# Halved query scaling, held token scaling and an earlier channel mix in a four-layer network

## The chip, the cores and the metric

The kernel runs on one core of one Trainium2 chip. The metric is the device time of one execution in microseconds (us); before the change the median of three runs is 1311.0.

## The reference

`x` is 8 batches of 256 tokens of 256 features, the context 8 batches of 256 tokens of 192 features. All is fp32.

```python
x = x + xattn0(layernorm(x), ctx, mask)     # 16 heads of 16
x = x + soft_moe(layernorm(x))              # 8 experts of 128 slots, hidden 1024, gelu
# second attention, 16 heads of 64:
h = layernorm(x)
q, k, v = h @ w_q, ctx @ w_k, ctx @ w_v     # 256 -> 1024, 192 -> 1024
x = x + softmax(q k^T / 8) v @ w_out + b_out
# channel mix:
h = layernorm(x)
prev = h shifted by one token (zero first)
xr = mu_r * h + (1 - mu_r) * prev
xk = mu_k * h + (1 - mu_k) * prev
x = x + sigmoid(xr @ W_r^T) * (relu(xk @ W_k^T) ** 2 @ W_v^T)
```

## The kernel before

Tokens lie on the 128 partitions: batch b is token tiles 2b and 2b+1 of the resident buffer `x_sb`. The stages follow one another: the first attention, the soft mixture of experts (until 866 us), the second attention (866 to about 1231 us) and the channel mix (to the end), with the later stages' first steps drawn into the earlier ones.

The first stages are left alone by the diff. The experts' matmuls `ph` (L1237) and `pe` (L1253) take turns, ACT reads `ph` (L1245), and the last matmuls `pc` (L1279) are added to `x_sb` by DVE (L1287). Then SP issues the loads of the weights of the last two layers (L1344 to L1359), at the very end the two small loads of `mu`, from which DVE makes `omu` = 1 - mu (L1361).

The second attention is a pipeline by steps. A step is one pair of heads of one batch, 64 steps in all; two steps make a group, and 36 rounds n = 0 to 35 run the 32 groups: `stage(k, g)` issues part k of group g. Part 0 is the scores and DVE's row maximum `nm` and ACT's exponentials `ex`; part 1 the reciprocal `rz` on DVE and the multiplication of `ex` on POOL (L1512); part 2 the transposes `pe` and their copies `et` (L1529, alternately by DVE and ACT); part 3 the products with V; part 4, after a batch's last step, the projection `po`. In a round, parts 3, 2 and 1 of earlier groups are issued in that order around two lists of extra pieces, `between[n]` and `ahead[n]`, written out by hand: for batch b, `normed_of(b)` scales the tokens with their mean and root (`xh_l`, two DVE operations of L106), `turned_of(b)` transposes them (`pt_x`, copied to `xT`) and adds the output bias to `x_sb` on POOL (L1411), `queries_of(b, t2)` makes the queries of four heads, `keys_of` and `values_of` the keys and values.

A query piece, `q_piece`, is four matmuls into one PSUM tile `pq` of 128x512 (one of three buffers of that size that all such tiles share): two for heads t = 2 t2 and two for t = 2 t2 + 1, each with 256 columns. Each fp32 matmul shows as two passes in the profile. Then one DVE operation (L1429) scales all 512 columns into `QT`. There are 32 such pieces.

Order within an engine: all matmuls and transposes are kept in program order. On DVE, ACT and POOL a scheduler may move an operation ahead of others if it is not marked. `Ordered` is a wrapper of DVE and POOL, used by `normed` and by the iterated roots: what is issued through it while `Ordered.held` is true keeps its place in program order. In before this was so for the tokens of channel mix batches 0 and 1 and the iterated roots, not for `xh_l`.

The channel mix of batch b has five pieces, `mixes[b][0]` to `[4]`: [4] scales the tokens (`xh_ffn`), [0] transposes them (`pt_xf`) and blends them with their shifted copy by `mu` on ACT (L1636) and `omu` on DVE (L1639), [1] makes the keys (`pk`), [2] the gates (`pr`, sigmoid on ACT), [3] the values (`pv`), the product, the addition of `x_sb` and the store. Roots of the variances: batches 0 to 3 by a Newton iteration (`first_roots`), batches 4 to 6 by ACT's square root and a DVE reciprocal (`mix_roots`, L1750), batch 7 by iteration (`last_roots`).

Of the kernel before, what the change touches and what calls it, by code (L numbers as in the profile page):

```python
# [15 lines left out]
P = 128  # L16
# [50 lines left out]
def kernel(ctx: ExitStack, tc: tile.TileContext, a: dict, out: bass.AP):  # L67
# [1266 lines left out]
    with ExitStack() as l1:  # L1334
# [61 lines left out]
        def proj1(b):  # L1396

            to = {}  # L1400

            def normed_piece():
                mv, rstd = xat_stats[b // 2]
                to["xh"] = normed(b, mv, rstd, "l1", of=4)

            def xt_piece():
                pt = transposed(to["xh"], f"x1_{b}", transpose)
                to["xT"] = p1.tile([P, 2, S], F32, tag="xT", bufs=1, name=f"xT1_{b}")
                nc.vector.tensor_copy(to["xT"], pt)
                for t in range(2):  # L1410
                    nc.gpsimd.tensor_tensor(  # L1411
                        x_sb[:, 2 * b + t, :], x_sb[:, 2 * b + t, :], bo, ALU.add
                    )

            def q_piece(t2):
                if t2 == 0:
                    to["QT"] = p1.tile([P, 8, S], F32, tag="QT", bufs=2, name=f"QT1_{b}")
                pq = ps_mm(f"q1_{b}_{t2}").rearrange("p (t n) -> p t n", t=2)
                for i in range(2):
                    t = 2 * t2 + i  # L1420
                    for c in range(2):
                        matmul(
                            pq[:, i, :],
                            lhsT=wq[:, c, t * P : (t + 1) * P],
                            rhs=to["xT"][:, c, :],
                            start=(c == 0),
                            stop=(c == 1),
                        )
                nc.vector.tensor_scalar(  # L1429
                    to["QT"][:, 2 * t2 : 2 * t2 + 2, :], pq, HD1**-0.5, None, ALU.mult  # L1430
                )

            def values_of(u):

                if u == 0:
                    to["V"] = p1.tile([P, 2, DA], F32, tag="V", bufs=2, name=f"V1_{b}")
                pv = [ps_mm(f"v1_{b}_{u}_{h}") for h in range(2)]
                t0 = S * b + u * P
                cols = [slice(h * 512, (h + 1) * 512) for h in range(2)]
                for h in range(2):  # L1440
                    matmul(
                        pv[h],
                        lhsT=ctx0T[:, t0 : t0 + P],
                        rhs=wv[:, 0, cols[h]],
                        start=True,
                        stop=False,
                    )

                def halves():
                    for h in range(2):  # L1450
                        r = slice(64 * h, 64 * h + 64)
                        matmul(
                            pv[h],
                            lhsT=ctx1T[r, t0 : t0 + P],
                            rhs=wv[r, 1, cols[h]],
                            start=False,
                            stop=True,
                        )
                    nc.scalar.copy(to["V"][:, u, cols[0]], pv[0])
                    nc.vector.tensor_copy(to["V"][:, u, cols[1]], pv[1])  # L1460

                return halves

            return (
                to,
                [lambda t=t: q_piece(t) for t in range(4)],
                [lambda u=u: values_of(u) for u in range(2)],
                normed_piece,
                xt_piece,
            )  # L1470
# [122 lines left out]

        normed_of(0)()
        turned_of(0)()
        normed_of(1)()
        keys_of(0, 0)()
        queries_of(0, 0)()
        xat_stats[3] = ln_pair(3, "xat_3")
        keys_of(0, 1)()  # L1600
        queries_of(0, 1)()
# [14 lines left out]
        def channel_mix(b):  # L1616
            xh = []

            def mix_normed():
                mv, rstd, of = ffn_stats[b]  # L1620
                Ordered.held = b < 2
                xh.append(normed(b, mv, rstd, "ffn", of=of))
                Ordered.held = False

            def mix():
                if b >= 2:
                    mix_normed()
                st = homes[b % 2]
                yT = yTs[b % 2]
                pt = transposed(xh[0], f"xf_{b}", transpose)  # L1630
                nc.vector.tensor_copy(yT[:, :, 1 : S + 1], pt)
                for k, n in enumerate(("r", "k")):
                    m = st[n].rearrange("p (c n) -> p c n", c=2)
                    for c in range(2):
                        i = 2 * k + c
                        nc.scalar.activation(  # L1636
                            m[:, c, :], yT[:, c, 1 : S + 1], AF.Copy, scale=mu[:, i : i + 1]
                        )
                        nc.vector.scalar_tensor_tensor(  # L1639
                            m[:, c, :],  # L1640
                            yT[:, c, 0:S],
                            omu[:, i : i + 1],
                            m[:, c, :],
                            ALU.mult,
                            ALU.add,
                        )
# [95 lines left out]
            root_step(rstd, v, t)  # L1742
            Ordered.held = False

        def mix_roots(b, of):

            mv, rstd = halves[b // 4]
            part = slice(2 * b % 8, 2 * b % 8 + 2 * of)
            tc.keep_in_program_order(
                nc.scalar.activation(rstd[:, part], mv[:, part, 1], AF.Sqrt, bias=epsb)  # L1750
            )
            nc.vector.reciprocal(rstd[:, part], rstd[:, part])

        def last_roots(b):

            mv, rstd = halves[b // 4]
            part = slice(2 * b % 8, 2 * b % 8 + 2)
            v = stat.tile([P, 8], F32, tag="nv", bufs=1, name=f"nv_ffn_{b}")[:, :2]
            Ordered.held = True
            vec.tensor_scalar(v, mv[:, part, 1], EPS, None, ALU.add)  # L1760
            inverse_root(rstd[:, part], v, f"ffn_{b}")
            Ordered.held = False
# [1 line left out]
        mixes = [channel_mix(b) for b in range(B)]  # L1764
        between = {n: [] for n in range(len(groups) + 4)}
        ahead = {n: [] for n in range(len(groups) + 4)}
        between[1] += [keys_of(0, 2), queries_of(0, 2), queries_of(0, 3), turned_of(1)]
        between[2] += [queries_of(1, 0)]
        ahead[2] += [keys_of(0, 3), values_of(0, 0), values_of(0, 1)]
        between[3] += [queries_of(1, 1)]  # L1770
        ahead[3] += [keys_of(1, 0)]
        between[4] += [queries_of(1, 2), queries_of(1, 3), normed_of(2), turned_of(2)]
        ahead[4] += [keys_of(1, 1), values_of(1, 0)]
        between[5] += [queries_of(2, 0), queries_of(2, 1)]
        ahead[5] += [keys_of(1, 2), values_of(1, 1)]
        between[6] += [queries_of(2, 2)]
        ahead[6] += [normed_of(3), keys_of(1, 3), values_of(2, 0)]
        between[7] += [queries_of(2, 3), turned_of(3)]
        ahead[7] += [values_of(2, 1)]
        for n in range(8, len(groups)):  # L1780
            b, i = n // 4 + 1, n % 4
            if b < B:
                between[n].append(queries_of(b, i))
            if i == 3 and b + 1 < B:
                between[n].append(turned_of(b + 1))
            if i == 2 and b + 1 < B:
                ahead[n].append(normed_of(b + 1))
            if i < 2 and n // 8 < B // 2 - 1:
                ahead[n].append(keys_of(n // 8 + 1, n % 8 // 4 * 2 + i))
            elif i >= 2 and b < B:  # L1790
                ahead[n].append(values_of(b, i - 2))
        for n in range(len(groups) + 4):
# [3 lines left out]
            for piece in between[n]:  # L1796
                piece()
            for k in (1, 2) if n < 28 else (2, 1):
                stage(k, n - k, slice(1, 2))
            if n - 4 != 27:  # L1800
                stage(4, n - 4)
            for piece in ahead[n]:
# [3 lines left out]
                mix_stats(n // 4 - 2, n % 4)  # L1806
            if 22 <= n < 25:
                first_roots(n - 22)
            if n in (30, 31):
                mixes[n - 30][4]()  # L1810
            if n == 32:
                homes_of_mix()
                mixes[0][0]()
                stage(4, 27)
                mixes[1][0]()
                for t in range(2):
                    mix_stats(6, t)
                mix_roots(4, 3)
            if n == 33:
                mixes[0][1]()  # L1820
                mixes[0][2]()
            if n == 34:
                mixes[1][1]()
        for t in range(2):
            mix_stats(7, t)
        last_roots(7)
        mixes[1][2]()
        for b in range(2, B + 2):
            if b < B:
                mixes[b][0]()  # L1830
            if 3 <= b <= B:
                mixes[b - 1][1]()
                mixes[b - 1][2]()
            mixes[b - 2][3]()
# [62 lines left out]
```

## Time and profile before

| | us |
|---|---|
| median of 3 runs | 1311.0 (1310.98 to 1312.02) |
| profiled execution | 1311.15 |
| its span | 1309.0 |
| busy PE | 1288.0, 98% of the span |
| busy ACT, DVE | 583.8 and 568.7 |
| busy POOL | 264.6 |
| granted PE clock, mean | 0.999 |

The span is the profiled part of the execution; 2.15 us lie around it. PE is the tensor engine's matmuls, PEld its weight loads, DVE the vector engine, ACT the scalar engine, POOL the general engine, SP the engine that issues the loads and stores. A row of the timeline gives the start, the duration, the engine, the line of the kernel, the operation, output and inputs, partitions by elements, how often it follows on itself, and in brackets the idle time of the engine ahead of it with what ended it. A row of groups gives busy time and mean ns of one, then idle time ahead and its main cause.

### The profile page before, as it was taken

What the parts mean: (1) busy time and instruction counts of PE and PEld (TensorE: products, weight loads), DVE (VectorE), ACT (ScalarE), POOL (GpSimd) and SP (SyncE); (2) the same over time, 40 slices, a digit from 0 to 9 for tenths busy, and PEclk for the clock granted to TensorE, in tenths of its full rate; (3) what the DMA queues carried; (4) which work ended last, traced back from release to release, by engine and by line L of the source; (5) the groups of instructions that cost most, each with busy time, mean ns of one, the idle gap of its engine ahead of it and who ended that gap; (6) DMA issues with size and microseconds to landing.
All of it is one profiled execution on the core that took longest, in us unless ns stands there. A gap on an engine that the chain in (4) does not pass through costs nothing.

```text
span 1309.0 us, 19001 instructions
## 1 busy us (share of the span) xinstructions
PE 1288.0 (98%) x7459; PEld 943.0 (72%) x7459; DVE 568.7 (43%) x1121; ACT 583.8 (45%) x1425; POOL 264.6 (20%) x322
## 2 busy tenths in 40 slices
PE   9999999999999999999999999999999999999998
PEld 6656555676778787787877888875666677677777
DVE  6778767243310333303333010035545535544855
ACT  4755556363521445414443232224445445544843
POOL 4563112110100010000101000023334233233523
PEclk9999999999999999999999999999999999999999
DMA  7001000242442332334322344250000000000001
GB/s 217 7 1 34 33 1 2 101 137 69 137 136 72 135 137 69 105 101 137 111 95 71 135 137 139 102 157 1 1 1 1 1 1 1 1 1 1 2 9 57
DMA packets 59144, 86.84 MB, mean 66 GB/s; under 512 B 3248, under 2 KB 49200, under 8 KB 59056
## 3 DMA queue, kind: packets, MB, share of 16 engines
q1 hardware_dynamic: 58560, 85.18, 19.8%
q8 instruction: 59, 0.97, 0.3%
q10 hardware_dynamic: 496, 0.46, 0.1%
q14 instruction: 29, 0.24, 0.1%
HBM read 83.53 MB, written 2.10 MB: 65 GB/s over the span
## 4 chain that ended last, share of the span: by engine, by line
PE 91%; ACT 4%; DVE 3%; POOL 1%; DMA 1%; issue 1%; SPq 0%; ACTq 0%; DVEq 0%; POOLq 0%
PE ph L1237 17%; PE pe L1253 16%; PE sc L77 9%; PE o L77 6%; PE po L77 6%; PE q L77 5%; PE v L77 5%; PE pe L80 4%; PE pc L1279 4%; PE k L77 4%; PE ln L1101 3%; PE pf L1183 3%; PE ln L77 1%; PE pk L77 1%; ACT ex L652 1%; PE pf L77 1%
## 5 line engine op out<-in xcount | busy, mean ns | idle before, releaser
L1245 ACT ACTIVATE ht<-ph,b 128x256 f32<-128x256 f32 x256 | 119.3, 474 | 377.1 <-PE ph L1237 371.7
L1237 PE MATMUL ph<-slots,w 128*128 128x256 f32 x1024 | 266.6, 384 | 1.2 <-ACT ht L1245 0.6
L1253 PE MATMUL pe<-w,ht 128*128 128x256 f32 x1024 | 263.2, 381 | 0.0
L1237 PEld LDWEIGHTS ph<-slots,w 128*128 128x128 f32 x1024 | 182.4, 189 | 53.8 <-ACT ht L1245 21.5
L1253 PEld LDWEIGHTS pe<-w,ht 128*128 128x128 f32 x1024 | 192.1, 190 | 29.9 <-DVE slots L1262 4.2
L1512 POOL TENSOR_TENSOR ex<-ex,rz 128x1024 f32<-128x1024 f32 x64 | 120.4, 1897 | 233.4 <-DVE rz L1510 200.4
L1499 ACT ACTIVATE ex<-sc,nm 128x256 f32<-128x256 f32 x256 | 117.4, 484 | 52.1 <-DVE nm L1494 50.4
L1161 POOL TENSOR_TENSOR es<-es,zs 128x1024 f32<-128x1024 f32 x12 | 22.7, 1895 | 429.6 <-DVE zs L1160 429.6
L652 ACT ACTIVATE ex<-sc 128x512 f32<-128x512 f32 x128 | 75.3, 598 | 65.2 <-PE sc L77 57.6
L1262 DVE TENSOR_TENSOR slots<-pe,b 128x512 f32<-128x512 f32 x32 | 22.1, 692 | 185.1 <-PE pe L1253 185.1
L106 DVE TENSOR_REDUCE NM<-sc 128x2 f32<-128x512 f32 x128 | 86.7, 688 | 23.0 <-PE sc L77 19.3
L77 PE MATMUL sc<-KT,QT 64*128 64x256 f32 (+2 forms) x896 | 93.7, 380 | 0.7 <-DVE NM L106 0.5
L77 PEld LDWEIGHTS sc<-KT,QT 64*128 64x128 f32 (+2 forms) x896 | 69.5, 186 | 20.6 <-issue 13.2
L1494 DVE TENSOR_REDUCE nm<-sc 128x4 f32<-128x1024 f32 x64 | 75.4, 1220 | 7.8 <-PE sc L77 4.2
L77 PE MATMUL po<-wo,ot 128*128 128x256 f32 x320 | 73.5, 384 | 0.3 <-ACT et L1529 0.3
L80 PE MATMUL pe<-ident,ex 128*128 128x128 f32 x512 | 69.0, 278 | 1.9 <-DVE et L1529 1.9
L80 PEld LDWEIGHTS pe<-ident,ex 128*128 128x128 f32 x512 | 56.6, 141 | 18.5 <-issue 13.7
L77 PEld LDWEIGHTS po<-wo,ot 128*128 128x128 f32 x320 | 59.5, 190 | 12.1 <-issue 2.7
L77 PE MATMUL o<-et,V 128*64 128x256 f32 x512 | 62.3, 385 | 0.0
L77 PE MATMUL q<-xT,wq 128*128 128x256 f32 x256 | 60.4, 381 | 0.0
L1279 PE MATMUL pc<-slots,CT 128*128 128x256 f32 x256 | 57.5, 379 | 0.0
L1499 ACT ACTIVATION_READ_ACCUMULATOR ex<-sc,nm 128x1 f32 x256 | 55.2, 216 | 0.0
(259 smaller groups left out, 1708.0 us busy)
## 6 DMA issues: line engine op xcount, KB each, us to landing
w<-in_w_dram SPq DMA_DIRECT2D x64, 1024.0 KB, 6.3
b<-in_b_dram SPq DMA_DIRECT2D x32, 128.0 KB, 6.7
x_sb<-in_x_dram SPq DMA_DIRECT2D x3, 512.0 KB, 7.8
se<-in_slots_dram SPq DMA_DIRECT2D x1, 1024.0 KB, 11.8
wq<-in_wq_dram SPq DMA_DIRECT2D x1, 1024.0 KB, 4.7
wo<-in_wo_dram SPq DMA_DIRECT2D x1, 1024.0 KB, 11.3
ctx1T<-in_ctxT_dram SPq DMA_DIRECT2D x7, 128.0 KB, 7.0
ctx0T<-in_ctxT_dram SPq DMA_DIRECT2D x3, 256.0 KB, 7.3
```

Source lines behind the costliest of these rows:

```text
L77: tc.keep_in_program_order(nc.tensor.matmul(out, lhsT=lhsT, rhs=rhs, start=start, stop=stop))
L80: tc.keep_in_program_order(nc.tensor.transpose(out, in_, ident))
L106: ins = op(*args, **kwargs)
L652: nc.scalar.activation(ex[:, 2 - 2 * i : 4 - 2 * i, :], sc[1 - i][:, :, 1, :], AF.Exp)
L1101: nc.tensor.matmul(pl[:, m * 512 : (m + 1) * 512], lhsT=st["xnT"][:, c, t * P : (t + 1) * P], rhs=snT[:, c, m * 512 : (m + 1) * 512], star ...
L1237: nc.tensor.matmul(ph, lhsT=c_["w1"][:, c, hc * P : (hc + 1) * P], rhs=slots[e][:, c * 256 : (c + 1) * 256], start=(c == 0), stop=(c == 1),)
L1245: nc.scalar.activation(ht, ph, AF.Gelu, bias=b1[:, e, hc : hc + 1])
L1253: nc.tensor.matmul(c_["pe"][:, b, :], lhsT=c_["ht"][hc][:, b * SL : (b + 1) * SL], rhs=c_["w2"][:, hc, :], start=(hc == 0), stop=(hc == HI ...
L1279: nc.tensor.matmul(pc[:, :D], lhsT=CT[:, bl, e, t * P : (t + 1) * P], rhs=eos[e][:, bl, :], start=(e == 0), stop=(e == E - 1),)
L1494: nc.vector.tensor_reduce(nm, sc, AX.X, ALU.max, negate=True)
L1499: nc.scalar.activation(ex[:, i, qb, :], sc[:, i, qb, :], AF.Exp, bias=nm[:, i, qb : qb + 1], accum_out=z[:, i, qb : qb + 1],)
L1512: nc.gpsimd.tensor_tensor(ex, ex, rz.rearrange("p h q -> p (h q)").unsqueeze(2).to_broadcast([P, 4, S]), ALU.mult,)
```

## The change

Six edits:

1. `q_piece` scales each half of `pq` (two heads, 256 columns) as soon as its two matmuls are issued, in place of one scaling of 512 columns.
2. `xh_l` of every batch is held in program order.
3. `normed_of(1)` goes behind the first keys and queries; `normed_of(b)` moves from `ahead` to the round's middle in the other rounds, for batch 2 one round earlier.
4. Part 1 of the second step of group 0 is issued in the middle of round 1, ahead of two query pieces.
5. The channel mix scales every batch's tokens a round before it transposes them; transposes and gates of its first batches are issued in earlier rounds.
6. The roots of batches 4 to 6 are iterated by `last_roots` too; ACT's square root is left out.

```diff
             def normed_piece():
                 mv, rstd = xat_stats[b // 2]
+                Ordered.held = True
                 to["xh"] = normed(b, mv, rstd, "l1", of=4)
+                Ordered.held = False
...
-                nc.vector.tensor_scalar(
-                    to["QT"][:, 2 * t2 : 2 * t2 + 2, :], pq, HD1**-0.5, None, ALU.mult
-                )
+                    nc.vector.tensor_scalar(to["QT"][:, t, :], pq[:, i, :], HD1**-0.5, None, ALU.mult)
...
         normed_of(0)()
         turned_of(0)()
-        normed_of(1)()
         keys_of(0, 0)()
         queries_of(0, 0)()
+        normed_of(1)()
...
             def mix_normed():
                 mv, rstd, of = ffn_stats[b]
-                Ordered.held = b < 2
+                Ordered.held = True
...
             def mix():
-                if b >= 2:
-                    mix_normed()
...
-        def mix_roots(b, of):
-
-            mv, rstd = halves[b // 4]
-            part = slice(2 * b % 8, 2 * b % 8 + 2 * of)
-            tc.keep_in_program_order(
-                nc.scalar.activation(rstd[:, part], mv[:, part, 1], AF.Sqrt, bias=epsb)
-            )
-            nc.vector.reciprocal(rstd[:, part], rstd[:, part])
-
-        def last_roots(b):
+        def last_roots(b, of):
...
-        between[1] += [keys_of(0, 2), queries_of(0, 2), queries_of(0, 3), turned_of(1)]
+        between[1] += [keys_of(0, 2), lambda: stage(1, 0, slice(1, 2))]
+        between[1] += [queries_of(0, 2), queries_of(0, 3), turned_of(1)]
...
-        between[3] += [queries_of(1, 1)]
+        between[3] += [queries_of(1, 1), normed_of(2)]
...
-        between[4] += [queries_of(1, 2), queries_of(1, 3), normed_of(2), turned_of(2)]
+        between[4] += [queries_of(1, 2), queries_of(1, 3), turned_of(2)]
...
-        between[6] += [queries_of(2, 2)]
-        ahead[6] += [normed_of(3), keys_of(1, 3), values_of(2, 0)]
+        between[6] += [queries_of(2, 2), normed_of(3)]
+        ahead[6] += [keys_of(1, 3), values_of(2, 0)]
...
             if i == 2 and b + 1 < B:
-                ahead[n].append(normed_of(b + 1))
+                between[n].append(normed_of(b + 1))
...
-                stage(k, n - k, slice(1, 2))
+                if (k, n) != (1, 1):
+                    stage(k, n - k, slice(1, 2))
...
-            if n in (30, 31):
-                mixes[n - 30][4]()
+            if n in (29, 30):
+                mixes[n - 29][4]()
             if n == 32:
                 homes_of_mix()
                 mixes[0][0]()
                 stage(4, 27)
+            if n == 33:
                 mixes[1][0]()
+                mixes[0][1]()
+                mixes[0][2]()
+                mixes[2][4]()
+            if n == 34:
+                mixes[1][1]()
+                mixes[2][0]()
+                mixes[1][2]()
+                mixes[3][4]()
                 for t in range(2):
                     mix_stats(6, t)
-                mix_roots(4, 3)
-            if n == 33:
-                mixes[0][1]()
-                mixes[0][2]()
-            if n == 34:
-                mixes[1][1]()
-        for t in range(2):
-            mix_stats(7, t)
-        last_roots(7)
-        mixes[1][2]()
-        for b in range(2, B + 2):
+                last_roots(4, 3)
+        mixes[0][3]()
+        for b in range(3, B + 2):
             if b < B:
                 mixes[b][0]()
-            if 3 <= b <= B:
+            if b == 3:
+                for t in range(2):
+                    mix_stats(7, t)
+                last_roots(7, 1)
+            if b + 1 < B:
+                mixes[b + 1][4]()
+            if b <= B:
                 mixes[b - 1][1]()
                 mixes[b - 1][2]()
             mixes[b - 2][3]()
```

More of the change, by code (lines that the diff above doesn't have):

```diff
@@ L1743, in first_roots @@
             Ordered.held = False
-        def mix_roots(b, of):
+        def last_roots(b, of):
             mv, rstd = halves[b // 4]
             part = slice(2 * b % 8, 2 * b % 8 + 2 * of)
-            tc.keep_in_program_order(
-                nc.scalar.activation(rstd[:, part], mv[:, part, 1], AF.Sqrt, bias=epsb)
-            )
-            nc.vector.reciprocal(rstd[:, part], rstd[:, part])
-        def last_roots(b):
-            mv, rstd = halves[b // 4]
-            part = slice(2 * b % 8, 2 * b % 8 + 2)
-            v = stat.tile([P, 8], F32, tag="nv", bufs=1, name=f"nv_ffn_{b}")[:, :2]
+            v = stat.tile([P, 8], F32, tag="nv", bufs=1, name=f"nv_ffn_{b}")[:, : 2 * of]
             Ordered.held = True
```

## The prediction

> **What bounds the kernel now.** I read the page first, its busy shares and the chain of waits, then the list of PE's waits from 880 us on, then the timeline of three stretches: around 866 us, where the second attention starts, around 978 us, in its steady part, and from 1231 us, the tail. The chain's shares by engine and two groups of the page:
>
> ```profile
> PE 91%; ACT 4%; DVE 3%; POOL 1%; DMA 1%; issue 1%; SPq 0%; ACTq 0%; DVEq 0%; POOLq 0%
> ...
> L1237 PE MATMUL ph<-slots,w 128*128 128x256 f32 x1024 | 266.6, 384 | 1.2 <-ACT ht L1245 0.6
> ...
> L77 PE MATMUL q<-xT,wq 128*128 128x256 f32 x256 | 60.4, 381 | 0.0
> ```
>
> PE is busy for 98% of the span and carries 91% of the chain: whatever makes PE wait is paid in full, and work of DVE, ACT or POOL counts only where PE waits for it. The third row is the one that the change touches: 256 passes of the query matmuls (an fp32 matmul is two passes) with no idle time ahead of any. The list of PE's waits from 880 us on shows how little there is to recover:
>
> ```profile
> PE pe L80 <- DVE et L1529: 1.9, 2, 1.5
> PE pk L77 <- DVE mix_home L1639: 1.0, 2, 0.8
> PE po L77 <- ACT et L1529: 0.3, 1, 0.3
> PE k L77 <- ACT et L1529: 0.2, 1, 0.2
> ```
>
> Columns: total, times, longest, in us. Measured by starts of passes rather than by modelled ends, PE loses 2.1 us in 888 to 895 and 2.9 us in 1236 to 1271 (0.53, 0.48, 0.41 and 1.46 at 1237.0, 1238.6, 1249.6 and 1269.8), and nothing between. So 5.0 us, 0.38% of 1311.15, is the most that a better order of work can bring from the second attention on. The smallest difference that a measurement of this kernel can tell from no change is about 0.2%, 2.6 us.
>
> **Part 1, queries scaled in halves.** One 128x512 scaling (L1429) of a query piece becomes two of 128x256, the first issued as soon as the first half's four passes are issued. Both halves lie in one PSUM tile of 128x512, and in the built order of the changed program the third matmul of every piece, the first that writes the second half, waits for DVE's scaling of the first half: 32 times of 32, where before there is no such wait. PE's queue has nothing else between the two halves, so all of it, that is the second half and whatever PE has behind it, stands still. The timeline of before shows the piece whole:
>
> ```profile
> 977.59 1.89 PE L77 MATMUL q<-xT,wq 128*128 128x256 f32 x8
> ...
> 979.52 0.69 DVE L1429 TENSOR_SCALAR QT<-q 128x512 f32<-128x512 f32 x1 [0.79 <-PE q L77]
> ```
>
> Eight passes 0.216 us apart, the last one 0.38 long; DVE starts 0.04 after it (979.48 to 979.52), as in 28 of the 32 pieces. With a wait in the middle, from the start of the fourth pass: 0.38 for the pass, 0.04 to DVE, 0.42 for a 128x256 operation of DVE out of PSUM (L1698 in the rows below; L1287, with one more operand, takes 0.48), 0.05 until PE runs on (a `pe` transpose starts that long after the DVE copy that it waited for, at 1236.99), less the 0.216 that a pass takes anyway. That is 0.67 us. The first pass after a stall takes some 0.10 more than in a stream (at 1270.72, 0.32 to the next start against 0.216, its weights not being loaded behind another pass). So 0.77 us a piece, times 32: **+24.8 us**. The three rows, from the tail's timeline:
>
> ```profile
> 1236.99 0.66 PE L80 MATMUL pe<-ident,ex 128*128 128x128 f32 x4 [0.37 <-DVE et L1529]
> ...
> 1270.72 1.56 PE L77 MATMUL pk<-mix_home,sb_wkT 128*128 128x256 f32 x6 [0.23 <-DVE mix_home L1639]
> ...
> 1302.73 0.42 DVE L1698 TENSOR_TENSOR mix_home<-mix_home,pv 128x256 f32<-128x256 f32 x1 [3.74 <-PE pv L77]
> ```
>
> From below, without that 0.10: 21.6. From above, with a reciprocal (0.17) still on DVE ahead of the scaling and 0.48 instead of 0.42: 1.0 a piece, 32 us. I take 0.77, since DVE stood idle when 28 pieces ended and the small reciprocal ahead of many of them ends near the half's end. The second half's scaling ends 0.27 earlier than the whole one did, but no PE pass waits for it.
>
> The row of L1237 is the nearest precedent: there too a second half waits for ACT's reading of the first half of its bank, and PE loses only 1.2 us in 1024 passes, because passes of `pe` (L1253) stand between. Nothing stands between here, so its price, near zero, is the low end only if the order were another.
>
> [...]
>
> **Part 2, token scaling held in program order.** `xh_l` of batch 0 was done early, during the experts. Held, it stands on DVE right behind `omu` (L1361), which stands behind the last `x_sb` (L1287) and needs both mu loads. These are issued last, behind some 5 MB of weights:
>
> ```profile
> 863.39 1.22 SPq L1358 DMA_DIRECT2D mu<-in_mu_r_dram  x1
> 864.65 1.26 SPq L1359 DMA_DIRECT2D mu<-in_mu_k_dram  x1
> ...
> 865.99 0.60 PE L80 MATMUL pt_x<-ident,xh_l 128*128 128x128 f32 x4
> ...
> 867.39 0.72 DVE L106 TENSOR_SCALAR xh_l<-x_sb,mvp_xat,rstdp_xat 128x256 f32<-128x256 f32 x2
> ...
> 873.85 0.66 DVE L1361 TENSOR_SCALAR omu<-mu 128x4 f32<-128x4 f32 x1
> ...
> 885.87 2.28 DVE L106 TENSOR_SCALAR xh_l<-x_sb,mvp_xat,rstdp_xat 128x256 f32<-128x256 f32 x2
> ```
>
> The DMA list gives 8.0 and 7.0 us from issue to landing, 871.4 and 871.67. Today `omu` runs late at 873.85 and nobody waits for it. In the new order `omu`, `xh_l` and the transposes `pt_x`, PE's first work of the stage, follow one on another: 871.67, 0.04 to DVE, 0.17 (a tiny DVE operation such as `rz`; the 0.66 above was beside a POOL addition), 0.72 for the two `xh_l`, 0.05 to PE: 872.65 in place of 865.99, **+6.65 us**. Bounds: 6.3 if the transposes of the first token tile start after one `xh_l`; 7.15 with 0.66 for `omu`. Queued on DVE behind `omu` are also the statistics of the last pair and the query scalings; all come later than `pt_x` anyway. SP's order of issues is unchanged.
>
> PE's clock is the second price. The last stretch of before reads (busy of PE, PEld, DVE, ACT, POOL, then the granted clock):
>
> ```profile
> 1303.00:1309.00 6.00, 2.12 (x10) 1.52 (x8) 2.60 (x7) 0.00 (x0) 0.73 (x1) 0.88 0.26 87
> ```
>
> The clock falls to half 2.4 us after the last pass. At the start, 128x128 passes are 0.213 us apart until 7.0 us and 0.109 later, that is full speed comes 5.2 us after the first pass at 1.82. Stretches of 3.4 us with PE busy by half its passes (887.7 to 891.1) keep the full clock. An idle PE from 866.2 to 872.65 is longer than 2.4 us, so I count on half speed when work resumes; at 5.2 us of it 2.6 us are lost, with the restoring edge on the same 3.41 us spacing as the two edges seen (7.03 and 1307.51, 381 of them apart) it comes at 877.4, 4.8 us on. I take **+2.4 us**, from 0 (the clock stays) to 3.4.
>
> [...]
>
> The later `xh_l` move from ahead of a round to its middle, and those of batches 1 and 2 by up to a round. From POOL's `ex` to the transposes that need it lie 6 to 14 us in the steady part, so 0.72 us of DVE there costs nothing; without that cover each of seven would cost at most 0.72, 5 us in all.
>
> **Part 3, the early rounds.** `rz` of the second step comes earlier (its stage is moved ahead of two query pieces), and the `xh_l` of 2.28 us at 885.87 is no longer ahead of the `nm` and `et` that PE waited for at 891.16. The 2.1 us of stalls there go: **-2.1**, at least 1.4.
>
> **Part 4, the tail.** The scalings `xh_ffn` go a round ahead; `pt_xf` and a gate matmul come earlier, before the last projection; the ACT square root and its table load and reload (1.28 each) leave; three batches' roots are iterated instead, with 12 POOL operations of about 0.33 (4 us) and 3 DVE ones of 0.17, begun rounds before their use. The `po` wait at 1238.6 for ACT's `et` remains, and about 0.3 at the last `pe`. At 1269.8 the transposed tokens are ready sooner, but batch 7's statistics and roots now stand ahead of batch 4's tokens on DVE and POOL, worth some 0.6. Of 2.9 us I leave 2.0: **-0.9**, from 0 to -2.0. The end itself, last pass, two additions and the store, is unchanged.
>
> **Sum.** 1311.15 + 24.8 + 6.65 + 2.4 - 2.1 - 0.9 = 1342.0 for the profiled execution; the median of the runs, 1311.0, lies 0.15 lower, so **1341.8 us**.
>
> **Rivals.**
> - Only the start is slower: the wait between halves costs nothing, as at L1237. 1311.0 + 6.65 + 2.4 - 2.1 - 0.9 = 1317.0. For it: DVE idles 0.79 us ahead of that scaling. Against: no PE work between the halves. 0.06.
> - Only the halves cost: the mu loads land before 866, or `omu` doesn't hold `xh_l`. 1311.0 + 24.8 - 3.0 = 1332.8. Against: landings at 871.4 and 871.67 with the queue in the same order. 0.06.
> - The clock stays at full: 1339.4, inside the range and counted in the forecast's chance.
> - Faster: the added waits find their releasers done, and the order recovers the idle of PE. With s for a piece and d for the start, the difference is 32 s + d - 3.0, so it needs 32 s + d under 3.0: even with s at zero the mu loads would have to land by 868.6. At zero for both, with the full 5.0 recovered, 1306.0. The row of L1237 speaks for it, the landings against. 0.03, and 0.02 for within 0.2%.
>
> The forecast holds 0.83. Its bounds: 21.6 + 6.3 + 0 - 2.1 - 2.0 gives 1334.7, and 32 + 7.15 + 3.4 - 1.4 - 0 gives 1352.2; both extremes at once are unlikely at the top, and 1334 to 1350 leaves out the rivals and little else.
>
> **What would show it.** In the profile after: the group of `q` with some 20 to 25 us of idle ahead of it put down to DVE `QT`, 64 scalings of 0.42; `pt_x` starting near 872.6 behind `omu`; passes twice as far apart until about 877; no stall at 891; the rest of the second attention as before. It would be wrong if `q` shows no idle, if `pt_x` starts at 866, or if DVE's queue, at 43% busy, makes PE wait in places not named here.

## The result and the profile after

The changed kernel takes 1339.78 us (median of 5 runs, 1337.40 to 1340.84), before 1311.21: ratio 1.0215, 95% interval 1.0201 to 1.0229. It is slower by 28.6 us; 1341.8 was predicted, 1334 to 1350 as the range. The profiled execution took 1340.84, its span 1338.8.

From the page after, the chain's shares by engine, and the group of the query matmuls (idle time ahead of them, with its cause, is the last part):

```profile
PE 87%; DVE 6%; ACT 3%; DMA 2%; issue 1%; POOL 1%; SPq 0%; ACTq 0%; DVEq 0%; POOLq 0%
...
L77 PE MATMUL q<-xT,wq 128*128 128x256 f32 x256 | 68.9, 394 | 17.3 <-DVE QT L1431 17.3
```

PE gave up four points of the chain, to DVE three and to a DMA one. The query group, which had no idle time, has 17.3 us. That figure is counted to the modelled end of the pass before; by starts of passes the loss is larger. The list of PE's waits from 860 us on holds most of the result (what the slow clock costs is no wait and does not stand in it):

```profile
PE q L77 <- DVE QT L1431: 17.3, 32, 1.3
PE pt_x L80 <- DVE xh_l L106: 6.4, 1, 6.4
PE po L77 <- ACT et L1529: 0.8, 1, 0.8
PE pt_xf L80 <- DVE xh_ffn L106: 0.3, 1, 0.3
```

The first row has one wait for each of the 32 pieces, the second is the start of the second attention, the last two are the new waits of the tail; those of before for `et` at 891 and for `mix_home` at 1270 are gone. A piece in the steady part (timeline):

```profile
947.11 1.03 PE L77 MATMUL q<-xT,wq 128*128 128x256 f32 x4
...
948.18 0.42 DVE L1431 TENSOR_SCALAR QT<-q 128x256 f32<-128x256 f32 x1
...
948.65 1.99 PE L77 MATMUL q<-xT,wq 128*128 128x256 f32 x8 [0.52 <-DVE QT L1431]
```

Four passes, 0.42 us of DVE, 0.05 later PE goes on. By starts, 31 of the 32 pieces lose 0.68 us in the middle and 0.10 at the next pass; one, at 904.24, loses 1.46, because DVE was still at two `et` copies and a reciprocal. The start of the stage:

```profile
873.42 0.17 DVE L1361 TENSOR_SCALAR omu<-mu 128x4 f32<-128x4 f32 x1 [5.33 <-DMA mu<-in_mu_k_dram]
873.50 0.73 DVE L106 TENSOR_SCALAR xh_l<-x_sb,mvp_xat,rstdp_xat 128x256 f32<-128x256 f32 x2
...
873.96 1.22 PE L80 MATMUL pt_x<-ident,xh_l 128*128 128x128 f32 x4 [6.39 <-DVE xh_l L106]
...
874.97 3.62 PE L77 MATMUL k<-ctx0T,wk 128*128 128x512 f32 x4
```

The load of `mu`, `omu`, the token scaling, the transposes, as the prediction had them. Four `k` passes take 3.62 us where they took 1.88 before: the clock is at half. The same in stretches of time (length, then busy PE, PEld, DVE, ACT, POOL, then the granted clock, DMA share and GB/s):

```profile
867.00:874.00 7.00, 0.61 (x4) 0.21 (x2) 1.06 (x4) 0.00 (x0) 0.01 (x1) 0.70 0.83 256
874.00:880.00 6.00, 6.00 (x12) 2.35 (x12) 0.92 (x2) 0.00 (x0) 1.50 (x2) 0.50 0.01 3
```

### The profile page after: what moved, and what is told of

Read it like the earlier page. It is cut to its first block, busy times and chain, and to the rows that moved or that the text cites. A ratio compares the mean times of both kernels' runs of the same rounds, so it can differ in the third digit from the quotient of the medians.

```text
span 1338.8 us, 19048 instructions
## 1 busy us (share of the span) xinstructions
PE 1296.1 (97%) x7459; PEld 940.9 (70%) x7459; DVE 566.5 (42%) x1155; ACT 582.1 (43%) x1423; POOL 268.9 (20%) x334
## 4 chain that ended last, share of the span: by engine, by line
PE 87%; DVE 6%; ACT 3%; DMA 2%; issue 1%; POOL 1%; SPq 0%; ACTq 0%; DVEq 0%; POOLq 0%
PE ph L1237 17%; PE pe L1253 16%; PE sc L77 9%; PE o L77 6%; PE po L77 5%; PE v L77 4%; PE k L77 4%; PE q L77 4%; PE pe L80 4%; PE pc L1279 3%; PE pf L1183 3%; PE ln L1101 3%; DVE et L1529 2%; PE pf L77 1%; PE ln L77 1%; ACT ex L652 1%
## 5 line engine op out<-in xcount | busy, mean ns | idle before, releaser
L1237 PE MATMUL ph<-slots,w 128*128 128x256 f32 x1024 | 266.6, 384 | 1.2 <-ACT ht L1245 0.6
L1237 PEld LDWEIGHTS ph<-slots,w 128*128 128x128 f32 x1024 | 182.4, 189 | 53.8 <-ACT ht L1245 21.5
L77 PE MATMUL q<-xT,wq 128*128 128x256 f32 x256 | 68.9, 394 | 17.3 <-DVE QT L1431 17.3
L77 PEld LDWEIGHTS q<-xT,wq 128*128 128x128 f32 x256 | 43.7, 190 | 36.4 <-DVE QT L1431 30.2
```

What stands on the lines that cost most here:

```text
L77: tc.keep_in_program_order(nc.tensor.matmul(out, lhsT=lhsT, rhs=rhs, start=start, stop=stop))
L1237: nc.tensor.matmul(ph, lhsT=c_["w1"][:, c, hc * P : (hc + 1) * P], rhs=slots[e][:, c * 256 : (c + 1) * 256], start=(c == 0), stop=(c == 1),)
```

## The experiments

The theory: the 32 waits come from the two halves sharing one PSUM tile; the start waits for `mu` through `omu`; the passes after it are slow because PE had stood idle. The rivals: the number of DVE operations, the held order as such, the loads still under way. Each version has runs of before beside it (their median is 1311.3 to 1311.8); the intervals are those of the ratio to before.

**One scaling again.** In the changed kernel, all else left:

```diff
-                    nc.vector.tensor_scalar(to["QT"][:, t, :], pq[:, i, :], HD1**-0.5, None, ALU.mult)
+                nc.vector.tensor_scalar(
+                    to["QT"][:, 2 * t2 : 2 * t2 + 2, :], pq, HD1**-0.5, None, ALU.mult
+                )
```

> The changed kernel with one 128x512 scaling of each query piece again; all other edits stay. Theory (the wait between the halves of one PSUM tile): the 32 stalls of 0.68 us in front of the third matmul and the 0.10 us behind each go, 25.9 us; 3.4 us of small delays at first passes elsewhere, which the changed kernel does not show, may come back. So 1314 to 1317.5, with the 6.6 us of idle ahead of pt_x and the slow clock behind it still there. Rival (the 32 additional DVE operations load DVE, and PE would wait somewhere for DVE even without the wait in the middle): the same drop, so this run alone does not tell the two apart. Second rival (the stalls only move to another wait for DVE, as the pieces follow one another): less than 10 us come back, 1330 or more.

Measured: 1318.10 us, ratio 1.0051 (1.0036 to 1.0065). No stall is left in a query piece. The halves are worth 21.7 us net, and 6.3 of the slowdown stay. It lies 0.6 above what was expected.

**The split alone.** The kernel of before with only the first edit of the change:

> The kernel of before with the two scalings in halves and nothing else. Theory: the wait costs by itself, without the other edits: 32 times 0.70 to 0.81 us, so 1333.5 to 1337, no idle ahead of pt_x, the stall of 1.7 us at 891 still there or covered by the new stalls. Rival (the loss needs the held token scalings, which stand ahead of the scalings on DVE): under 1325.

Measured: 1334.61 us, ratio 1.0175 (1.0161 to 1.0189). 31 stalls of 0.68 again and one of 3.27 us (there DVE had two `nm` reductions and two `et` copies still ahead of the half's scaling, late behind a token scaling of 2.28; behind that stall the clock stood at half for 3.4 us). The split needs none of the other edits to cost what it costs.

**Two scalings, behind all four matmuls.** In the changed kernel:

```diff
-                    nc.vector.tensor_scalar(to["QT"][:, t, :], pq[:, i, :], HD1**-0.5, None, ALU.mult)
+                for i in range(2):
+                    nc.vector.tensor_scalar(
+                        to["QT"][:, 2 * t2 + i, :], pq[:, i, :], HD1**-0.5, None, ALU.mult
+                    )
```

> The changed kernel with two 128x256 scalings for each piece, but both issued behind all four matmuls of the piece. The number of DVE operations is that of the changed kernel. Theory (wait in the middle): the stalls go, as no matmul of a piece waits for a scaling of the same piece; within 1 us of the version with one scaling. Rival (number of DVE operations, DVE load): within 5 us of the changed kernel's 1339.8.

Measured: 1320.65 us, ratio 1.0068 (1.0056 to 1.0081). The number of DVE operations is cleared: the 32 stalls are gone with as many operations. But it is 2.5 us above the version with one scaling, not within 1: the two together take 0.76 us where one took 0.69, and the passes behind a piece came later by that. This was the first sign that PE does wait for the end of the scaling.

**Banks of their own.** In the changed kernel, a tile for each half:

```diff
-                pq = ps_mm(f"q1_{b}_{t2}").rearrange("p (t n) -> p t n", t=2)
                 for i in range(2):
                     t = 2 * t2 + i
+                    pq = ps_mm(f"q1_{b}_{t2}_{i}")[:, :S]
...
-                            pq[:, i, :],
+                            pq,
...
-                    nc.vector.tensor_scalar(to["QT"][:, t, :], pq[:, i, :], HD1**-0.5, None, ALU.mult)
+                    nc.vector.tensor_scalar(to["QT"][:, t, :], pq, HD1**-0.5, None, ALU.mult)
```

> The changed kernel with each half of a query piece in a PSUM tile of its own (two of the three buffers that such tiles share), each scaled as soon as its two matmuls are issued. Theory (it is the shared bank that makes the third matmul wait): no stall between the halves; the buffers turn faster, and now and then a matmul waits for the reading of the tile three back, 0 to 4 us in all. So 0 to 4 us above the version with one scaling, 1314 to 1321. Rival (early scalings themselves disturb, by DVE's order): near 1339.8.

Measured: 1313.91 us, ratio 1.0018 (1.0008 to 1.0029). The group of the query matmuls (page):

```profile
L77 PE MATMUL q<-xT,wq 128*128 128x256 f32 x256 | 60.7, 381 | 0.3 <-DVE et L1529 0.3
```

The same early scalings, the same 64 of them, and 17.3 us of idle have become 0.3: it is the shared tile. Tile and bank change together here, so no run tells the two apart. And it is 4.2 us better than one scaling, where 0 to 4 worse was expected. Small delays, under 0.15 us each, are why. In before a piece is followed by eight transposes and then by `k` or `v` matmuls into the buffer that the piece just used (the tiles of the transposes take the other two of the three). Of the timeline, first before, then the version with banks of its own and the first tokens free (below):

```profile
979.32 1.04 PE L80 MATMUL pe<-ident,ex 128*128 128x128 f32 x8
...
980.27 1.98 PE L77 MATMUL k<-ctx0T,wk 128*128 128x512 f32 x4
```

```profile
977.37 1.04 PE L80 MATMUL pe<-ident,ex 128*128 128x128 f32 x8
978.25 1.88 PE L77 MATMUL k<-ctx0T,wk 128*128 128x512 f32 x4
```

From the transposes to `k` it is 0.95 us before and 0.88 after, and the four passes take 1.98 and 1.88. In before the 128x512 scaling, shown with the prediction, runs from 979.52 to 980.21, and `k` starts 0.06 later; its second pass loses another 0.10. The scaling of the last 256 columns alone is done 0.27 us sooner, and the delay is gone. With half scalings, in one tile or two, such delays vanish: 17 pieces are followed by eight transposes and `k` or `v`, and by starts of passes before takes 0.94 us or more from the transposes to the first pass and 0.53 to the second behind each of them, the changed kernel 0.87 and 0.43. With banks of their own alone, from 980.86, it is 0.88, and the four passes take 1.88.

**The halves with banks of their own, alone.** The kernel of before with the scaling in halves and a tile for each half, and nothing else:

> The kernel of before with only the query scaling in halves, each in a PSUM tile of its own. Theory (in before, the 128x512 scaling ends just too late for the k and v matmuls that use its tile next, which costs 0.08 to 0.18 us a piece): 3.5 to 5 us less than before, 1306.5 to 1308.5. Rival (these small delays belong to the change of operand and have nothing to do with the scaling): no change, 1310.5 to 1312.5, or slower by the faster turn of the tiles.

Measured: 1308.85 us, ratio 0.9977 (0.9966 to 0.9988). Faster by 2.9 us, 0.35 short of the range expected. In its profile PE gains 3.9 us on before between 898 and 1231 us, by the small delays alone, so the delays do belong to the scaling. But in one early piece a stall of 2.28 us opened, and behind it the clock stood at half for 3.4 us: 888 to 898 takes 1.6 us more than before, though the stall of 1.7 at 891 is gone.

**`omu` later.** In the changed kernel, issued behind the second query piece (the expectation calls it the fourth):

```diff
-        nc.vector.tensor_scalar(omu, mu, -1.0, 1.0, ALU.mult, ALU.add)
...
         keys_of(0, 1)()
         queries_of(0, 1)()
+        tc.keep_in_program_order(nc.vector.tensor_scalar(omu, mu, -1.0, 1.0, ALU.mult, ALU.add))
```

> The changed kernel with omu issued behind the fourth query piece's place instead of right behind the loads, so that on DVE it no longer stands ahead of the first token scaling; that scaling stays held and stands directly behind the last x_sb. Theory (pt_x waited for the mu loads through omu): pt_x starts as soon as the last x_sb and two scalings are done, 1.4 us behind the last pass of pc instead of 6.6 to 7.6, and with so short an idle time PE's clock stays at full, which gives back another 2.5 to 3.1. Together 7.5 to 9 us less than the changed kernel's 1339.8: 1331 to 1332.5. Rival (the token scaling waits for something else, the statistics or the last x_sb): pt_x starts near 873 as before and the time stays within 1.5 us of 1339.8.

Measured: 1330.85 us, ratio 1.0148 (1.0132 to 1.0165), 8.9 less than the changed kernel. Its timeline:

```profile
866.39 0.73 DVE L106 TENSOR_SCALAR xh_l<-x_sb,mvp_xat,rstdp_xat 128x256 f32<-128x256 f32 x2
...
866.85 0.87 PE L80 MATMUL pt_x<-ident,xh_l 128*128 128x128 f32 x4 [0.90 <-DVE xh_l L106]
867.55 1.88 PE L77 MATMUL k<-ctx0T,wk 128*128 128x512 f32 x4
```

The scaling is held as before, but only the last `x_sb` is ahead of it: 0.90 us of wait, and `k` at full speed. It was the load of `mu` ahead of the scaling, not the holding by itself.

**The idle time filled.** In the changed kernel, ahead of the first `pt_x`; the added transposes compute nothing that is used:

```diff
         normed_of(0)()
+        idle = ps_o("idle").rearrange("p (i n) -> p i n", n=P)
+        for i in range(56):
+            transpose(idle[:, i % 4, :], ident)
         turned_of(0)()
```

> The changed kernel with 56 transposes of the identity, about 6.1 us of them, in PE's queue ahead of the first pt_x, where PE stands idle; they write a tile that nobody reads. Theory (the passes behind the idle time are slow because PE stood idle): pt_x starts as before near 873, but its passes lie 0.109 apart and those of k 0.43, not 0.85; 2.5 us less than the changed kernel, near 1337.3. Rival (they are slow for another reason, such as the weights still coming in, or POOL's work): spacing and time unchanged, 1339.8.

Measured: 1338.20 us, ratio 1.0203 (1.0187 to 1.0219). The timeline and a stretch of time:

```profile
866.94 6.28 PE L80 MATMUL idle<-ident 128*128 128x128 f32 x56
874.80 0.87 PE L80 MATMUL pt_x<-ident,xh_l 128*128 128x128 f32 x4 [1.58 <-DVE xh_l L106]
875.50 1.88 PE L77 MATMUL k<-ctx0T,wk 128*128 128x512 f32 x4
```

```profile
875.00:880.00 5.00, 4.50 (x16) 1.94 (x15) 1.87 (x4) 0.58 (x1) 1.33 (x2) 1.00 0.00 0
```

With the loads as they were, the clock stays at 1.00 and `k` takes 1.88: it was the idle time that made it slow. The gain in time is 1.6 instead of 2.5, too small to be told from the spread of both kernels' runs; in this execution `mu` also came later, so `pt_x` started 1.3 us later after the last `pc` than in the changed kernel.

**The early rounds alone.** The kernel of before with edits 2 (batch 0 left free), 3 and 4:

> The kernel of before with only the token scalings held (batch 0 left free) and the changed order of the early rounds. Theory: the stalls of 1.7, 0.2 and 0.3 us at 891 to 894 go and nothing comes in their place: PE's waits from 880 us on are those of the tail alone, about 2 us less, 1309.5. Rival (the stalls went only because the changed kernel starts late and waits in every query piece, so that DVE runs ahead): a stall of over 1 us between 885 and 900 stays, time unchanged at 1311 to 1312.

Measured: 1309.51 us, ratio 0.9982 (0.9972 to 0.9992). PE's waits from 860 us on:

```profile
PE pk L77 <- DVE mix_home L1641: 1.0, 2, 0.8
PE pe L80 <- DVE et L1531: 0.4, 1, 0.4
PE po L77 <- ACT et L1531: 0.3, 1, 0.3
```

Only the tail's are left; by starts the 2.15 us at 891 became 0.23.

**The tail alone.** The kernel of before with edits 5 and 6:

> The kernel of before with only the edits of the channel mix and its roots. Theory: the waits of the tail become those of the changed kernel (one of about 0.9 us ahead of po, 0.4 and 0.2 ahead of pt_xf, 0.2 ahead of pe) in place of 0.53, 0.48, 0.41 and 1.46: 0.9 to 1.1 us less, 1310.5, less than the spread of the runs, so that the waits of the profile decide. Rival (the po wait of 0.9 comes from the late start): at 0.5 as before, and 1.4 us less.

Measured: 1310.53 us, ratio 0.9994 (0.9984 to 1.0005), not to be told from no change by time. By starts the stalls of the tail fell from 2.79 to 1.92 us, with the 0.93 ahead of `po` as in the changed kernel, so that wait has nothing to do with the late start.

**The change put right.** All six edits, with banks of their own for the halves (edited as above) and batch 0's token scaling left free:

```diff
-                Ordered.held = True
+                Ordered.held = b > 0
                 to["xh"] = normed(b, mv, rstd, "l1", of=4)
```

> All edits of the change, with two put right: each half of a query piece has a PSUM tile of its own, and the token scaling of batch 0 is not held. Theory: against the version with banks of its own (1313.9), the 7.3 us of idle ahead of pt_x and 3.1 us of slow clock go: 1303 to 1305, faster than before by 0.5 to 0.7%. This holds the gain of the halves (their tile is free 0.17 us or more before the next matmul into it is due, 4.5 us over all), and of the early rounds and the tail (3 us). Rival (the gain of the halves came from the late start, which let DVE run ahead): 1308 to 1311.

Measured: 1304.43 us (1304.07 to 1306.25), ratio 0.9944 (0.9932 to 0.9957): faster than both kernels, and than before by 7.3 us. PE's waits from 860 us on:

```profile
PE po L77 <- ACT et L1529: 0.8, 1, 0.8
PE q L77 <- DVE et L1529: 0.3, 1, 0.3
PE pt_xf L80 <- DVE xh_ffn L106: 0.3, 1, 0.3
```

## Why the prediction was right, and where it was off

The steps against the profiled executions, by starts of passes; the first and last pass lie 29.7 us further apart than before:

| step | predicted | measured |
|---|---|---|
| wait between the halves | +24.8 | +25.9 |
| end of the scaling earlier | 0 | -4.2 |
| idle time ahead of `pt_x` | +6.65 | +6.6 |
| slow clock and late first passes behind it | +2.4 | +3.05 |
| early rounds | -2.1 | -2.15 |
| tail | -0.9 | -0.87 |
| clock before 866 us | not there | +1.4 |

That 1339.8 lies only 2.0 below 1341.8 is in part luck: the -4.2 that the prediction left out stands against +1.1, +0.65 and +1.4.

**Halves.** The mechanism and the price of one piece stand (0.78 for 0.77): 31 times 0.78, and one piece at 1.46 with 0.10 behind it. The shared tile as the cause is shown by the runs with two scalings behind all matmuls and with banks of their own. The waits come to 17.3 us with one tile and to 0.3 with two.

**The step that failed** is the sentence that the second half's scaling ends 0.27 earlier "but no PE pass waits for it". PE does, at `k`, `v` and other users of the tile, by some 0.17 us at a time (in the lines above 0.07 at the first pass of `k` and 0.10 at its second), too short for the list of waits, which counts from modelled ends. The -4.2 is what the other rows leave; summing the small delays by kind of pass gives about -4. The low price of the nearest row, L1237, did not carry over, since the passes behind a piece cover the scaling of 0.69 us only almost.

**Start.** `pt_x` after `omu` and both loads, 6.6 us in this execution, 7.2 to 7.6 in three other kernels with the same start (one scaling, two scalings, banks of their own): the sum by one execution's landing was near its lower end. The 3.05 us behind it are two things. The first passes of `pt_x` come late behind the wait, which costs 0.27 even where the clock stays at full (`omu` later, filled idle time: the four take 0.87 us, in before 0.60). The slow clock is the other 2.8, 0.4 above its term. By the trace's record of the granted clock, half speed lasted from 869.78 to 880.02 us, 6.1 us of it behind the start of `pt_x`, not 4.8; in the three other kernels it was 4.8 to 5.0, at a cost of 2.1 to 2.2. So the term had the right size, and the time at half speed after an idle stretch is not the same in every execution. The upper bound of 3.4 us is shown by no run: the four costs measured are 2.1 to 2.2 and 2.8.

**Tail.** The sum came out, its parts did not: the `po` wait grew from 0.48 to 0.93 instead of remaining, and the 0.53 ahead of `pe` went. That too is luck.

**Clock before 866 us.** The profile after has 1.4 us that lie ahead of all edits. The stretch 222 to 225 us, after and before:

```profile
222.00:225.00 3.00, 3.00 (x8) 0.77 (x6) 0.10 (x1) 0.57 (x2) 1.43 (x3) 0.56 0.00 0
```

```profile
222.00:225.00 3.00, 3.00 (x20) 1.55 (x18) 1.70 (x7) 1.53 (x4) 1.57 (x4) 1.00 0.00 0
```

PE waits 2.13 us for DVE at 219.7 in both; in one the clock then falls to half for 3.4 us, which costs 1.6 us (ahead of that the profile after is 0.2 us faster, hence the 1.4). It did in the profiles of the changed kernel, one scaling, filled idle time, own banks alone and the tail alone (granted clock 0.52 to 0.78 from 222 us to 225 or 226), and not in those of the other seven kernels (1.00). No edit reaches that place. The prediction counted on a fall behind more than 2.4 us of idle time; here 2.13 was enough in five profiles, and not in seven.

The trace notes the time of each change of the granted clock. In the profile after, half speed lasts 3.413 us here (221.25 to 224.66) and 10.240 us at the start of the stage, and full speed between them 645.119: 3 and 189 times 3.413. The two changes in the trace of before, at 7.03 and 1307.51, lie 1300.478 us apart, 381 times 3.413, so the 3.41 us spacing that the prediction counted with fits the changes of both traces. In the 3.41 us ahead of the fall (217.84 to 221.25) PE was busy for 1.55 us in the profile after; in before it was busy for 1.44 in the same stretch, and the clock stayed at 1.00. So the busy time of that stretch alone does not decide, and no run shows what does: none shifted the wait on purpose.

**Rivals.** The one with only the start slower (1317.0) did not happen; what it describes is the version with banks of its own, which came out 3 us lower, mostly by the term missed above. The rival that ends faster, 1306.0 at best, took the recoverable idle time for 5.0 us; with the small delays there were some 4 more, and the version put right is at 1304.43. Its condition has a slip: to cost no more than 3.0 us the loads would have had to land by 868.0 (871.67 less 3.65), not 868.6. Nothing rests on it.

## What to carry to other kernels

Reading out half a tile early can cost more than it wins if the tensor engine's next work writes the other half: here the same edit, against one scaling in the otherwise same kernel, cost 21.7 us net in one tile and won 4.2 in two (in the kernel of before it cost 22.9 and won 2.9). Other work queued between the halves hid the wait in the row of L1237 (1.2 us of idle time in 1024 passes). Before holding an operation in program order, look at what stands directly ahead of it and what that waits for; a tiny operation behind the last small load held up a whole stage for 6.6 us, and the slow clock and late passes behind it cost 3 more. And a stage that the list of waits calls free of stalls may still lose some 0.15 us in every round: compare the starts of passes with their pace, and work out when the tile that they write is read out.

## What the runs showed of the hardware

- A pass that starts just after a late release loses more than the lateness: `k` 0.07 late at its first pass and 0.10 more at its second, as behind the 32 stalls of the changed kernel's query pieces (0.10 each).
- An idle stretch of 2.13 us, a third of that ahead of `pt_x`, was followed by half speed in the profiles of five kernels and not in those of seven, at the same place of the same code; in the profile after this cost 1.6 us. PE had been busy there for 1.55 of the 3.41 us ahead of the fall, and in before, which kept full speed, for 1.44 of the same stretch. What decides is not shown.
- The spread of 1310.2 to 1315.4 us in the runs of before goes with the granted clock: its mean is 0.996 in every run above 1314 and 0.998 to 1.000 in the others. Where in those runs the clock fell is not shown, as only one of them has a profile.
- Two 128x256 scalings one behind the other take 0.76 us, one of 128x512 takes 0.69.
